# Layer 3 of a four-layer convolution kernel: one narrow mask for four heads, keys summed down the rows ahead of the scan on VectorE, q kept by rows as well

## The chip, the cores and the metric

One core of one Trainium2 chip runs the whole program in one launch. The metric is the device time of that core in microseconds. The kernel before took 3273.11 us, the median of three runs (3265.43 to 3276.16).

## The reference

The input x is 4 images of 256 channels by 48 by 48, all in f32. Four layers follow, each of them added to its own input, after a group normalisation over 32 groups:

- layer 0: a dilated 7x7 convolution to 128 channels, a 1x1 convolution to 49 maps, a softmax over them, and the weighted sum of the 49 shifted inputs;
- layer 1: a 3x3 convolution of the signs of the input with the signs of the weights;
- layer 2: a 3x3 convolution with weights rounded to three values;
- layer 3: linear attention in windows, in 8 heads of 32 channels. The change touches this layer alone.

```python
q = sigmoid(x Wq);  k = sigmoid(x Wk);  v = x Wv, each head's v divided by its norm
Ik  = integral(k)                   # sums over rows and columns
Ikv = integral(k[f] * v[g])
for w in (1, 2, 4):                 # window sizes 48, 24, 12
    wk  = box(Ik, 48 // w)          # the sum of k over the window about each point
    wkv = box(Ikv, 48 // w)
    attn = sum_d q[d] wkv[d, f]
    norm = sum_d q[d] wk[d]
    outs.append(attn / (norm + 1e-6))
out = Wout concat(outs) + bout
```

## The kernel before, in words

Layers 0 to 2 run image by image and fill the first 1390 us. Layer 3 begins as layer 2 of the last image ends, and projections of image 0 for it (`project_first`) already run beside that.

**The tiling of layer 3.** An image is cut into 6 bands of 8 rows (`RB`, `NRB`) and each band of keys into 3 squares of 16 columns (`KC`, `NKC`), so that a square of 8 by 16 keys fills 128 partitions. A block (`Block`) is one image b, one half `ct` of the channels (4 heads, `HG`) and one band of queries `rb`; `order` lists the 48 blocks, by image, then by half, then by band. One pass is the six blocks of one image and half. A block goes over the bands of keys that its widest window reaches, each in two halves of the columns (`tiles_of`): 8 to 12 tile steps for each block, 480 in all. Near steps, whose band of keys is at most one from the band of queries, are alternated with far ones.

**A tile step.** `scores` multiplies keys with queries on TensorE for four heads. The four heads make two pairs (`NPR`), each with a PSUM tile `s` of two banks. `masked` then makes the masked scores `sm` for up to three windows: `widest` (ScalarE, or VectorE for one pair of a far step) clips at zero, `middle` multiplies with the mask of the window of 24 on VectorE, and for near steps GpSimd (POOL) multiplies the result with the mask of the narrow window of 12. Before, each pair had its own `sm` tile (`room`, L1950), so that a near step had four narrow multiplications: two pairs by two key squares. Two steps later (`LAG`), `sums` multiplies the masked scores with v, into one accumulator for each window. `scores` and `sums` stand in TensorE's queue in the order scores of step n, sums of step n-2, side work, scores of step n+1.

**The norms.** `k_sums` (L1672), one job for each half of the channels, makes the windowed sums of the keys. It loads a band of keys `kf_d` into `kp`, whose rows are padded with zeros, runs a scan along the whole of it (two calls, `cs`), and takes for each window the difference of two shifted views (`pt`, three subtractions on VectorE). Then it sums down the rows: POOL adds to each row of `pt`, for all three windows at once, the row above (L1713 to L1719), carries the last row to the next band, and `pt` is stored to `kb_d`. `norms` loads two bands of such sums (`nhi`, `nlo`) and q (`nq`, from `q_d`), subtracts and multiplies by q on POOL, and sums over channels by a matmul; `ns` goes to `n_d`, is read back in another layout, inverted by `inverse` and stored to `r_d`.

**The end of a block.** `finish` stores the first half's result, `stage`, to `o_d`. For the second half `prepare` loads the first one's result as `o`, and the inverse norms, repeated over each head's channels, as `rc`, and multiplies `o` by `rc` on POOL; `finish` multiplies `stage` by `rc` on VectorE and applies `Wout`.

**Layouts.** Queries are held in the order (column, row), `p (w r)`, for the scores, and `q_d` has that order. Norms are computed in the order (row, column). So the q product in `norms` reads q with a stride of 8 elements, and both products with `rc` read `rc` with a stride of 48 elements.

**What sets the order.** All engines' calls stay in program order (`InOrder`). Side work (projections, `k_sums`, `norms`, `state`, `prepare`, `finish`) consists of generators that `advance` (L339) resumes once a step, in between two tile steps. A job that has POOL work first calls `pool_turn` (L369) with an estimated cost, `pool_op` (190 + 1.95 ns an element), and is put off while the step has no such time left. The main loop gives a step 3600 ns of it, less `far_time` (L2279), the estimate of that step's narrow masks. TensorE's time is given out likewise by `bank` and `turn`. `until` (L356) is otherwise: when something must be ready, such as block i-2 before block i begins, it calls `advance()` with no limit at all, over and over until it is:

```python
    def until(*keys):
        while not made.issuperset(keys):
            assert active
            advance()
```

Counters in `free` stand for buffers: one `cs`, two `o`, two `rc`.

Of the kernel before, what the change touches and what calls it, by code (L numbers as in the profile page):

```python
# [12 lines left out]
F32 = mybir.dt.float32  # L13
# [9 lines left out]
P = 128  # L23
# [4 lines left out]
RB = 8  # L28
# [219 lines left out]
def conv_preact_kernel(  # L248
# [71 lines left out]
    q_d = [dram.tile([C, HW], F32, tag=f"q{b}", name=f"q_d{b}") for b in range(B)]  # L320
    k_d = [dram.tile([C, HW], F32, tag=f"k{b}", name=f"k_d{b}") for b in range(B)]
# [105 lines left out]
    class Projection:  # L427
# [50 lines left out]
        def qk(self, g, a, name, mo):  # L478
# [26 lines left out]
            if name == "k":  # L505
                kt = self.scr.tile([P, NB], F32, tag="kt", name="kt")
                act.copy(kt.rearrange("p (c r x) -> p c r x", c=NKC, x=KC), rows)
            yield 1
            if name == "k":
                sync.dma_start(out=k_d[b][chans, cols], in_=kt)  # L510
            sync.dma_start(out=(q_d if name == "q" else kf_d)[b][chans, cols], in_=t)
# [1110 lines left out]
    with (  # L1622
# [4 lines left out]
        tc.tile_pool(name="smp", bufs=2 * (LAG + 1), reuse_waits="tile") as smp,  # L1627
# [27 lines left out]
        GAP = HALVES[0] + 1  # L1655
# [5 lines left out]
        carry = wts.tile([P, NCT, NW, W], F32, name="carry")  # L1661
# [10 lines left out]
        def k_sums(mo):  # L1672
# [14 lines left out]
            for at, (b, a) in enumerate(todo):  # L1687
# [3 lines left out]
                while step < loaded + FETCH + 1:  # L1691
                    yield 1
                yield from take("cs")
                cs = scr.tile([P, (RB + 1) * ROW], F32, tag="cs", name="cs", bufs=1)
                n = GAP + RB * ROW
                for i, j in ((0, n // 2), (n // 2, n)):
                    dve.tensor_tensor_scan(
                        cs[:, i:j],
                        kp[:, i:j],
                        kp[:, 0:1].to_broadcast([P, j - i]),  # L1700
                        cs[:, i - 1 : i] if i > 0 else 0.0,
                        ALU.add,
                        ALU.add,
                    )
                    yield 1
# [4 lines left out]
                for wi, h in enumerate(HALVES):  # L1710
                    dve.tensor_sub(pt[:, wi], shifted(cs, h - 1), shifted(cs, -h - 1))
                    yield 1
                free["cs"] += 1  # L1713
                for r in range(RB):
                    if r % 2 == 0:
                        yield from pool_turn(NW * W, 2)
                    if a > 0 or r > 0:
                        up = pt[:, :, r - 1, :] if r > 0 else carry[:, mo]
                        pool.tensor_add(pt[:, :, r, :], pt[:, :, r, :], up)  # L1719
                pool.tensor_copy(carry[:, mo], pt[:, :, RB - 1, :])  # L1720
                yield 1
# [8 lines left out]
        def norms(b, rb):  # L1730
# [4 lines left out]
            def load(ct):  # L1735
# [3 lines left out]
                qf = scr.tile([P, W, RB], F32, tag="nq", name="nq")  # L1739
                sync.dma_start(  # L1740
                    out=qf.rearrange("p w r -> p (w r)"),
                    in_=q_d[b][chans, rb * NB : (rb + 1) * NB],
                )
# [55 lines left out]
            act.copy(ns, ps[0 : D * NW, 0:NB])  # L1799
# [91 lines left out]
        class Block:  # L1891
# [48 lines left out]
            def masked(self, a, half, ss):  # L1940
# [9 lines left out]
                def room():  # L1950

                    t = smp.tile([P, SM_ROOM], F32, tag="sm", name="sm")
                    at, blocks_, views = 0, {}, {}
                    for wi in wis:
                        y0, y1 = rows_seen(wi, a, rb)
                        ps = self.parts(wi, a, half)
                        if wi == 0:
                            n = sum(p1 - p0 for _, p0, p1 in ps) * (y1 - y0)
                            block = t[:, at : at + 2 * n].rearrange("p (j n) -> p j n", j=2)
                            blocks_[wi] = block  # L1960
                            at, o = at + 2 * n, 0
                            for c, p0, p1 in ps:
                                m = (p1 - p0) * (y1 - y0)
                                views[wi, c] = block[:, :, o : o + m].rearrange(
                                    "p j (x r) -> p j x r", r=y1 - y0
                                )
                                o += m
                            continue
                        for c, p0, p1 in ps:
                            n = 2 * (y1 - y0) * (p1 - p0)  # L1970
                            views[wi, c] = t[:, at : at + n].rearrange(
                                "p (j x r) -> p j x r", j=2, r=y1 - y0
                            )
                            at += n
                    assert at <= SM_ROOM
                    return blocks_.get(0), views

                pairs = [room() for _ in ss]

                def times_mask(engine, wi, c, rows, cols, dst, src):  # L1980
# [5 lines left out]
                        dst, src, m.unsqueeze(1).to_broadcast([P, 2, ncol, nr])  # L1986
# [4 lines left out]
                def middle(s, room_):  # L1991
                    y0, y1 = rows_seen(1, a, rb)
                    for c, p0, p1 in parts_seen(1, half):
# [4 lines left out]
                        times_mask(dve, 1, c, (y0, y1), (p0, p1), room_[1][1, c], src)  # L1998

                def widest(engine, s, room_):  # L2000
                    n = room_[0].shape[2]
                    lo, hi = strip_columns(half) if full else (0, n)
                    if engine is act:
                        act.activation(room_[0], s[:, :, lo:hi], AF.Relu)
                    else:
                        dve.tensor_scalar_max(room_[0], s[:, :, lo:hi], 0.0)

                first, second = zip(ss, pairs)
# [42 lines left out]
            def sums(self, wi, a, half, sms):  # L2051
# [3 lines left out]
                for k, (c, p0, p1) in enumerate(self.parts(wi, a, half)):  # L2055
                    for j in range(HG):
# [5 lines left out]
                            sms[j // 2][wi, c][:, j % 2],  # L2062
# [24 lines left out]
        def prepare(i):  # L2087
# [34 lines left out]
        def finish(i, stage):  # L2122
# [156 lines left out]
        def far_time(i, a, half):  # L2279
# [4 lines left out]
            return 2 * sum(pool_op(2 * n) for n in columns(NW - 1, a, half, rb))  # L2284
# [79 lines left out]
```

## Time and profile before

| what | value |
|---|---|
| median of three runs | 3273.11 us |
| the profiled execution's own time | 3273.94 us |
| its span, first to last instruction | 3272.1 us |
| mean granted TensorE clock | 0.955 |
| layer 3, from its first accumulator on | 1402.2 to 3272.1 us |
| PE, DVE, ACT, POOL busy in layer 3 | 1723, 1097, 693, 1434 us of 1870 |
| POOL, narrow masks (`sm<-sm,masks`) | 1024 operations, 685.9 us |
| POOL, sums down the rows (`pt<-pt`, `pt<-pt,carry`, `carry<-pt`) | 188.0, 21.7 and 18.2 us |
| POOL, norms (`nhi<-nhi,nq`) and divisions (`o<-o,rc`) | 176.2 and 87.8 us |

A row of a tile's view reads: line, engine, operation, output<-inputs, count, then the shortest, the median and the longest duration in ns, and the first and last start in us. All instructions carry one line, since a helper records them; so tiles tell them apart. A row of the view by stretches gives the stretch in us, its length, then the busy time and count of PE (matmuls), PEld (weight loads), DVE (VectorE), ACT (ScalarE) and POOL (GpSimd), the granted clock, the share of DMA and GB/s. A row of the waits reads: who waited, for whom, how many us in total, how many times, and the longest.

### The profile page before, as it was taken

To read this page: it belongs to the slowest core of one execution; us is meant where nothing else is said; L and a number is where in the kernel's file an instruction comes from. 1 tells how busy PE (TensorE), PEld (TensorE's weight loads), DVE (VectorE), ACT (ScalarE), POOL (GpSimd) and SP (SyncE) were. 2 spreads that over 40 slices of the span, in tenths; PEclk is the share of its full clock that TensorE was granted. 3 is DMA by queue.
4 is the path that set the end of the run, shared out by engine and by line. 5 is a ranking of instruction groups with operands and counts; after the bars stand their busy time and mean duration, and the time that the engine had idled before them with its cause. 6 is when DMAs were issued, how large, how long until landed. Compare 5 with 4: busy or idle time off the path is not lost.

```text
span 3272.1 us, 98025 instructions
## 1 busy us (share of the span) xinstructions
PE 2902.1 (89%) x41802; PEld 2004.4 (61%) x41802; DVE 2017.0 (62%) x3907; ACT 963.2 (29%) x1894; POOL 1613.6 (49%) x2658
## 2 busy tenths in 40 slices
PE   3678999899899978889986879998999999999999
PEld 2456777678677756756553536564656655666665
DVE  7886578648856632656675636665556665655555
ACT  0002210111121053245431224442335532333332
POOL 0000021003002130358999968989857888844554
PEclk9889899999999978989998989999999999999999
DMA  8746513332341243144554645354543354511322
GB/s 269 222 152 186 168 47 128 112 121 83 103 155 57 90 148 121 61 128 131 170 173 136 178 145 160 118 170 138 159 123 126 126 162 149 164 40 41 87 75 68
DMA packets 373126, 424.46 MB, mean 130 GB/s; under 512 B 129075, under 2 KB 328531, under 8 KB 371539
## 3 DMA queue, kind: packets, MB, share of 16 engines
q1 hardware_dynamic: 371491, 416.32, 41.1%
q8 instruction: 331, 5.42, 0.7%
q0 software_dynamic: 144, 1.08, 0.2%
q14 instruction: 104, 0.85, 0.1%
q10 hardware_dynamic: 1056, 0.79, 0.1%
HBM read 287.91 MB, written 131.25 MB: 128 GB/s over the span
## 4 chain that ended last, share of the span: by engine, by line
PE 51%; POOL 16%; DVE 10%; DMA 3%; ACT 3%; issue 3%; SPq 1%; ACTq 0%; POOLq 0%; DVEq 0%
PE cv L244 15%; PE s L244 13%; PE acc L244 11%; POOL sm L244 6%; PE out_ps L244 5%; PE proj_ps L244 4%; POOL nhi L244 4%; POOL pt L244 3%; PE ap L244 2%; DVE sm L244 2%; DVE l2v L244 2%; ACT sm L244 2%; SPq L244 1%; DVE v L244 1%; POOL vu L244 1%
## 5 line engine op out<-in xcount | busy, mean ns | idle before, releaser
L244 DVE TENSOR_TENSOR sm<-s,masks 128x448 f32<-128x448 f32 (+11 forms) x1536 | 632.6, 468 | 443.7 <-PE s L244 417.3
L244 POOL TENSOR_TENSOR sm<-sm,masks 128x352 f32<-128x352 f32 (+11 forms) x1024 | 685.9, 702 | 363.9 <-DVE sm L244 263.1
L244 ACT ACTIVATE sm<-s 128x384 f32<-128x384 f32 (+2 forms) x864 | 470.5, 545 | 845.3 <-PE s L244 662.2
L244 PE MATMUL acc<-sm,vs 128*32 128x128 f32 (+20 forms) x17920 | 626.1, 279 | 36.4 <-POOL sm L244 31.7
L244 PE MATMUL cv<-vx,wt 128*128 128x288 f32 x2080 | 562.8, 427 | 88.6 <-DVE vx L244 50.3
L244 PE MATMUL s<-qs,ks 32*128 32x192 f32 (+3 forms) x7680 | 594.3, 401 | 41.6 <-ACT sm L244 36.3
L244 PEld LDWEIGHTS acc<-sm,vs 128*32 128x32 f32 x17920 | 431.6, 110 | 241.9 <-issue 139.0
L244 PEld LDWEIGHTS s<-qs,ks 32*128 32x128 f32 x7680 | 372.7, 186 | 271.1 <-issue 122.3
L244 PEld LDWEIGHTS cv<-vx,wt 128*128 128x128 f32 x2080 | 404.7, 199 | 211.3 <-issue 52.7
L244 POOL MEMSET v<- 128x16 f32 (+1 forms) x120 | 18.7, 216 | 744.7 <-DVE vx L244 628.3
L244 PE MATMUL cv<-v,wl 128*128 128x384 f32 x1152 | 226.4, 357 | 25.2 <-DVE x L244 8.1
L244 PEld LDWEIGHTS cv<-v,wl 128*128 128x128 f32 x1152 | 216.4, 197 | 36.4 <-issue 16.7
L244 DVE TENSOR_SCALAR sm<-s 128x896 f32<-128x896 f32 (+1 forms) x96 | 111.1, 1157 | 186.1 <-PE s L244 161.2
L244 POOL TENSOR_TENSOR pt<-pt 128x144 f32<-128x144 f32 x336 | 188.0, 560 | 25.2 <-DVE pt L244 1.0
L244 POOL TENSOR_TENSOR nhi<-nhi,nq 128x384 f32<-128x384 f32 x144 | 176.2, 1243 | 0.0
L244 PE MATMUL s<-masks 24*128 24x192 bf16 (+2 forms) x1920 | 172.1, 269 | 0.0
L244 POOL TENSOR_TENSOR v<-l2v,v 128x384 fp32r<-128x384 f32 x96 | 109.0, 1166 | 117.4 <-ACT v L244 108.7
L244 PE MATMUL cv<-pad,wl 128*128 128x384 bf16 x864 | 145.6, 331 | 4.2 <-ACT pad L244 4.2
L244 PE MATMUL out_ps<-o,wout_sb 128*32 128x384 f32 x1152 | 123.8, 499 | 7.4 <-DVE res L244 3.4
L244 PE MATMUL out_ps<-stage,wout_sb 128*32 128x384 f32 x1152 | 123.5, 498 | 6.2 <-DVE stage L244 6.2
L244 PEld LDWEIGHTS <-wl 128*128 128x128 bf16 x864 | 84.5, 98 | 64.7 <-issue 7.2
L244 DVE SCALAR_TENSOR_TENSOR res<-out_ps,bout_sb,res 128x384 f32<-128x384 f32 x48 | 42.1, 878 | 128.9 <-PE out_ps L244 128.8
(174 smaller groups left out, 3515.1 us busy)
## 6 DMA issues: line engine op xcount, KB each, us to landing
wt<-wt SPq DMA_DIRECT2D x48, 768.0 KB
kb_d<-pt SPq DMA_DIRECT2D x48, 576.0 KB
rc<-r_d SPq DMA_DIRECT2D x192, 144.0 KB
nhi<-kb_d SPq DMA_DIRECT2D x120, 192.0 KB
nlo<-kb_d SPq DMA_DIRECT2D x88, 192.0 KB
o_d<-stage SPq DMA_DIRECT2D x24, 576.0 KB
o<-o_d SPq DMA_DIRECT2D x24, 576.0 KB
wl<-wl_d SPq DMA_DIRECT2D x16, 768.0 KB
```

What stands on the lines that cost most here:

```text
L244: return lambda *args, **kwargs: self.tc.keep_in_program_order(op(*args, **kwargs))
```

## The change

Everything is in layer 3.

- **One `sm` tile for both pairs.** `room` is gone; a step has one tile of twice the size (`smp` has `LAG + 1` buffers instead of twice that many), with views over four heads. `middle` and `widest` write a pair's slice of it. The narrow mask is one multiplication for four heads for each key square: two in a near step instead of four. `far_time` follows.
- **Sums down the rows first.** In `k_sums`, VectorE adds to each row of the keys `kp` the row above (48 elements, eight additions a band, in two groups of four with a step between), and keeps the last row in `carry`. The scan multiplies its running sum by a mask `inside`, which is zero ahead of each row and one elsewhere, and adds the keys. The padding of a row is 24 elements instead of 25. Where the lower end of a window lies left of the image, `pt` is a copy of the scan, made by ScalarE (25, 13 and 7 of 48 columns); VectorE subtracts in the others. POOL's additions, its carry and their `pool_turn`s are gone.
- **q by rows as well.** `qk` makes a second copy of q on ScalarE, in the order (row, column), and stores it to the new `qr_d`; `norms` loads that, and its product is flat. The copy of the norms out of PSUM (`ns`) now turns them to (column, row), so that the products of `o` and `stage` with `rc` are flat too.

```diff
@@ qk
-            if name == "k":
-                kt = self.scr.tile([P, NB], F32, tag="kt", name="kt")
-                act.copy(kt.rearrange("p (c r x) -> p c r x", c=NKC, x=KC), rows)
+            kt = self.scr.tile([P, NB], F32, tag="kt", name="kt")
+            pattern = "p (r c x) -> p c r x" if name == "q" else "p (c r x) -> p c r x"
+            act.copy(kt.rearrange(pattern, c=NKC, x=KC), rows)
             yield 1
-            if name == "k":
-                sync.dma_start(out=k_d[b][chans, cols], in_=kt)
-            sync.dma_start(out=(q_d if name == "q" else kf_d)[b][chans, cols], in_=t)
+            first, second = (qr_d, q_d) if name == "q" else (k_d, kf_d)
+            sync.dma_start(out=first[b][chans, cols], in_=kt)
+            sync.dma_start(out=second[b][chans, cols], in_=t)
@@ layer 3's pools and constants
-        tc.tile_pool(name="smp", bufs=2 * (LAG + 1), reuse_waits="tile") as smp,
+        tc.tile_pool(name="smp", bufs=LAG + 1, reuse_waits="tile") as smp,
-        GAP = HALVES[0] + 1
+        GAP = HALVES[0]
-        carry = wts.tile([P, NCT, NW, W], F32, name="carry")
+        carry = wts.tile([P, NCT, W], F32, name="carry")
+        inside = wts.tile([P, (RB + 1) * ROW], F32, name="inside")
+        nc.gpsimd.memset(inside, 1.0)
+        for r in range(RB + 1):
+            nc.gpsimd.memset(inside[:, r * ROW + GAP - 1 : r * ROW + GAP], 0.0)
@@ k_sums
+                keys = shifted(kp, 0)
+                for r in range(RB):
+                    if a > 0 or r > 0:
+                        up = keys[:, r - 1] if r > 0 else carry[:, mo]
+                        dve.tensor_add(keys[:, r], keys[:, r], up)
+                    if r % 4 == 3:
+                        yield 1
+                dve.tensor_copy(carry[:, mo], keys[:, RB - 1])
                 yield from take("cs")
...
                     dve.tensor_tensor_scan(
                         cs[:, i:j],
+                        inside[:, i:j],
                         kp[:, i:j],
-                        kp[:, 0:1].to_broadcast([P, j - i]),
                         cs[:, i - 1 : i] if i > 0 else 0.0,
-                        ALU.add,
+                        ALU.mult,
                         ALU.add,
                     )
...
-                    dve.tensor_sub(pt[:, wi], shifted(cs, h - 1), shifted(cs, -h - 1))
+                    ahead_, behind_ = shifted(cs, h - 1), shifted(cs, 0)
+                    act.copy(pt[:, wi, :, : h + 1], ahead_[:, :, : h + 1])
+                    dve.tensor_sub(
+                        pt[:, wi, :, h + 1 :], ahead_[:, :, h + 1 :], behind_[:, :, : W - h - 1]
+                    )
                     yield 1
                 free["cs"] += 1
-                for r in range(RB):
-                    if r % 2 == 0:
-                        yield from pool_turn(NW * W, 2)
-                    if a > 0 or r > 0:
-                        up = pt[:, :, r - 1, :] if r > 0 else carry[:, mo]
-                        pool.tensor_add(pt[:, :, r, :], pt[:, :, r, :], up)
-                pool.tensor_copy(carry[:, mo], pt[:, :, RB - 1, :])
-                yield 1
@@ norms
-                sync.dma_start(
-                    out=qf.rearrange("p w r -> p (w r)"),
-                    in_=q_d[b][chans, rb * NB : (rb + 1) * NB],
-                )
+                sync.dma_start(out=qf, in_=qr_d[b][chans, rb * NB : (rb + 1) * NB])
...
-                    pool.tensor_mul(hi[:, wi], hi[:, wi], qf.rearrange("p w r -> p r w"))
+                    flat = hi[:, wi].rearrange("p r w -> p (r w)")
+                    pool.tensor_mul(flat, flat, qf)
...
-            act.copy(ns, ps[0 : D * NW, 0:NB])
+            act.copy(
+                ns.rearrange("p (w r) -> p r w", w=W),
+                ps[0 : D * NW, 0:NB].rearrange("p (r w) -> p r w", w=W),
+            )
@@ masked
-                    for _, views in pairs:
-                        for c, p0, p1 in parts_seen(2, half):
-                            src = views[1, c][
-                                :, :, p0 - seen1[c] : p1 - seen1[c], y0 - z0 : y1 - z0
-                            ]
-                            times_mask(pool, 2, c, (y0, y1), (p0, p1), views[2, c], src)
-                return [views for _, views in pairs]
+                    for c, p0, p1 in parts_seen(2, half):
+                        src = views[1, c][:, :, p0 - seen1[c] : p1 - seen1[c], y0 - z0 : y1 - z0]
+                        times_mask(pool, 2, c, (y0, y1), (p0, p1), views[2, c], src)
+                return views
@@ prepare
-                ow = o[:, wi].rearrange("p (w r) -> p w r", w=W)
-                pool.tensor_mul(ow, ow, rcs[0][:, wi].rearrange("p (r w) -> p w r", w=W))
+                pool.tensor_mul(o[:, wi], o[:, wi], rcs[0][:, wi])
@@ finish
-                sw = stage[:, wi].rearrange("p (w r) -> p w r", w=W)
-                dve.tensor_mul(sw, sw, rc[:, wi].rearrange("p (r w) -> p w r", w=W))
+                dve.tensor_mul(stage[:, wi], stage[:, wi], rc[:, wi])
@@ far_time
-            return 2 * sum(pool_op(2 * n) for n in columns(NW - 1, a, half, rb))
+            return sum(pool_op(4 * n) for n in columns(NW - 1, a, half, rb))
```

More of the change, by code (lines that the diff above doesn't have):

```diff
@@ L320, in conv_preact_kernel @@
     q_d = [dram.tile([C, HW], F32, tag=f"q{b}", name=f"q_d{b}") for b in range(B)]
+    qr_d = [dram.tile([C, HW], F32, tag=f"qr{b}", name=f"qr_d{b}") for b in range(B)]
     k_d = [dram.tile([C, HW], F32, tag=f"k{b}", name=f"k_d{b}") for b in range(B)]
@@ L1738, in load @@
                 lo = scr.tile([P, NW, RB, W], F32, tag="nlo", name="nlo")
-                qf = scr.tile([P, W, RB], F32, tag="nq", name="nq")
-                sync.dma_start(
-                    out=qf.rearrange("p w r -> p (w r)"),
-                    in_=q_d[b][chans, rb * NB : (rb + 1) * NB],
-                )
+                qf = scr.tile([P, NB], F32, tag="nq", name="nq")
+                sync.dma_start(out=qf, in_=qr_d[b][chans, rb * NB : (rb + 1) * NB])
                 for wi, h in enumerate(HALVES):
@@ L1948, in masked @@
                 left = {c: x0 for c, x0, _ in PARTS[half]}
[L1950 to L1956, printed above, removed]
-                        if wi == 0:
[L1958 to L1967, printed above, removed]
-                            continue
[L1969 to L1976, printed above, removed]
@@ L1978, in masked @@
-                pairs = [room() for _ in ss]
+                t = smp.tile([P, NPR * SM_ROOM], F32, tag="sm", name="sm")
+                at, blocks_, views = 0, [], {}
+                for wi in wis:
+                    y0, y1 = rows_seen(wi, a, rb)
+                    ps = self.parts(wi, a, half)
+                    for c, p0, p1 in ps:
+                        if wi == 0:
+                            continue
+                        n = HG * (y1 - y0) * (p1 - p0)
+                        views[wi, c] = t[:, at : at + n].rearrange(
+                            "p (j x r) -> p j x r", j=HG, r=y1 - y0
+                        )
+                        at += n
+                    if wi > 0:
+                        continue
+                    n = sum(p1 - p0 for _, p0, p1 in ps) * (y1 - y0)
+                    block = t[:, at : at + HG * n].rearrange("p (j n) -> p j n", j=HG)
+                    blocks_ = [block[:, 2 * pr : 2 * pr + 2] for pr in range(NPR)]
+                    at, o = at + HG * n, 0
+                    for c, p0, p1 in ps:
+                        m = (p1 - p0) * (y1 - y0)
+                        views[wi, c] = block[:, :, o : o + m].rearrange(
+                            "p j (x r) -> p j x r", r=y1 - y0
+                        )
+                        o += m
@@ L1980, in times_mask @@
+                assert at <= NPR * SM_ROOM
                 def times_mask(engine, wi, c, rows, cols, dst, src):
@@ L1985, in times_mask, with middle @@
                     engine.tensor_mul(
-                        dst, src, m.unsqueeze(1).to_broadcast([P, 2, ncol, nr])
+                        dst, src, m.unsqueeze(1).to_broadcast([P, dst.shape[1], ncol, nr])
                     )
                 many = seen(NW - 1, a, rb)
-                def middle(s, room_):
+                def middle(s, pr):
                     y0, y1 = rows_seen(1, a, rb)
@@ L1997, in middle, with widest @@
                         )[:, :, :, y0:y1]
-                        times_mask(dve, 1, c, (y0, y1), (p0, p1), room_[1][1, c], src)
-                def widest(engine, s, room_):
-                    n = room_[0].shape[2]
+                        dst = views[1, c][:, 2 * pr : 2 * pr + 2]
+                        times_mask(dve, 1, c, (y0, y1), (p0, p1), dst, src)
+                def widest(engine, s, pr):
+                    dst = blocks_[pr]
+                    n = dst.shape[2]
                     lo, hi = strip_columns(half) if full else (0, n)
                     if engine is act:
-                        act.activation(room_[0], s[:, :, lo:hi], AF.Relu)
+                        act.activation(dst, s[:, :, lo:hi], AF.Relu)
                     else:
-                        dve.tensor_scalar_max(room_[0], s[:, :, lo:hi], 0.0)
-                first, second = zip(ss, pairs)
+                        dve.tensor_scalar_max(dst, s[:, :, lo:hi], 0.0)
+                first, second = zip(ss, range(NPR))
                 if full:
@@ L2061, in sums @@
                             kvs[self.b, self.ct, a][1][:, c, j, :],
-                            sms[j // 2][wi, c][:, j % 2],
+                            sms[wi, c][:, j],
                             start=(wi == 0 and (a, half) == todo[0] and k == 0),
```

## The prediction

> **What bounds the kernel now.** I read the page's totals and forty slices first, then the busy times by stage, then the engines' waits, then single tiles.
>
> ```profile
> span 3272.1 us, 98025 instructions
> PE 2902.1 (89%) x41802; PEld 2004.4 (61%) x41802; DVE 2017.0 (62%) x3907; ACT 963.2 (29%) x1894; POOL 1613.6 (49%) x2658
> PE   3678999899899978889986879998999999999999
> POOL 0000021003002130358999968989857888844554
> ```
>
> POOL's 49% is an average over two different programs. Up to slice 16 (layers 0 to 2) it is almost idle; in layer 3 it runs at 8 or 9 tenths, and PE dips where POOL is at 9. So I cut layer 3 into its eight passes (four images, two channel halves each), at the first clearing of the accumulators of each pass:
>
> ```profile
> core 0: us, PE busy (x) PEld busy (x) DVE busy (x) ACT busy (x) POOL busy (x), PEclk, DMA share, GB/s
> 1402.20:1627.90 225.70, 214.17 (x4813) 137.61 (x4812) 144.70 (x289) 114.75 (x230) 185.39 (x348) 0.97 0.43 135
> 1627.90:1944.70 316.80, 253.19 (x4585) 142.24 (x4584) 181.85 (x313) 79.40 (x158) 282.68 (x390) 0.92 0.54 158
> 1944.70:2166.50 221.80, 214.64 (x4616) 133.23 (x4608) 138.59 (x279) 105.29 (x209) 189.26 (x330) 1.00 0.47 141
> 2166.50:2416.60 250.10, 225.82 (x4594) 137.50 (x4592) 145.08 (x267) 78.12 (x159) 217.33 (x301) 0.97 0.55 161
> 2416.60:2630.50 213.90, 211.97 (x4646) 132.47 (x4639) 134.27 (x279) 108.17 (x216) 157.73 (x317) 1.00 0.37 117
> 2630.50:2868.60 238.10, 221.42 (x4526) 137.17 (x4528) 140.89 (x261) 74.27 (x148) 207.47 (x279) 0.98 0.54 158
> 2868.60:3056.50 187.90, 177.86 (x3975) 124.55 (x3968) 97.24 (x208) 67.90 (x134) 82.57 (x139) 1.00 0.13 42
> 3056.50:3272.00 215.50, 203.87 (x4198) 126.72 (x4196) 114.61 (x226) 64.72 (x124) 111.53 (x158) 1.00 0.28 81
> ```
>
> Matmul counts hardly differ, lengths do. The passes with 158 us of POOL or less are PE-bound (213.9 long, 212.0 busy). **The floor** of the others follows: between passes 5 and 7 a matmul is worth (213.9-187.9)/(4646-3975) = 0.0387 us. First-half floors are then 220, 213, 213; second-half floors start from the last pass (215.5 less some 6.5 of tail) plus 0.0387 per matmul more: 224, 224, 222. Against that the six passes lie 5, 93, 9, 26, 1 and 16 us too high: **150 us**.
>
> Most of it stands in three places, where a `begin` waits in the planner for an unfinished block (`until`) and the waiting steps are given out with no budget, so queued side jobs of POOL run one after another with no tile between them:
>
> ```profile
> 1747.00:1786.00 39.00, 20.91 (x235) 7.09 (x234) 17.01 (x21) 2.65 (x6) 36.90 (x44) 0.78 0.50 141
> 1900.30:1948.00 47.70, 29.69 (x264) 9.82 (x268) 9.14 (x11) 5.51 (x12) 29.16 (x31) 0.71 0.47 140
> 2233.00:2260.00 27.00, 15.99 (x150) 5.19 (x150) 6.95 (x11) 1.46 (x4) 25.77 (x37) 0.75 0.24 69
> ```
>
> POOL is busy 92 of these 114 us; the second also holds one 11 us wait for a load of key sums. PE's waits in layer 3 name the same owners, narrow masks and norms:
>
> ```profile
> PE acc L244 <- POOL sm L244: 31.7, 52, 2.1
> PE norm_ps L244 <- POOL nhi L244: 29.5, 18, 10.8
> ```
>
> [...] about half the operations that start with POOL in flight take longer:
>
> ```profile
> L244 DVE TENSOR_TENSOR pt<-cs x144: 541/644/1605, 1416.2 to 2703.5; 128x384 f32<-128x384 f32 x144
> L244 POOL TENSOR_TENSOR pt<-pt x336: 482/497/1074, 1418.4 to 2718.0; 128x144 f32<-128x144 f32 x168
> L244 DVE TENSOR_SCALAR nr<-nr x24: 184/471/1184, 1613.8 to 2873.5; 128x72 f32<-128x72 f32 x24
> ```
>
> [...] the trace's undisturbed ones are 541 to 550. [...] Here the q product (one operand strided by 32 bytes) has a median of 1197 ns against 1000 for the flat subtraction of the same size: 20%.
>
> **The change, part by part.** *Taken from POOL.* The row sums: 376 additions of 128x144 at 209.7 us (188.0+21.7) and 48 copies at 18.2: 228. Narrow masks, 1024 operations into 512 of twice the size: over their twelve sizes the medians lie on 0.22 us + 1.91 ns per element, so the fixed part goes 512 times: 114. The flat q product: 144 x 0.197 = 28. The flat o product: 72 x (1.244-1.039, the mean of the subtraction) = 15. Together 385 of POOL's 1434 us in layer 3; 1049 remain, 59% of some 1790. The planner follows: each row sum no longer asks it for four turns of two `pool_op(144)` (48 x 3.77 = 181 us of its units), and `far_time` gives back 0.38 per near step; norms and `prepare` are thus given out earlier.
>
> *Where that gain lies.* Of the 150 us I leave 35: the start's 5, and 10 at the end of each of three images, where `finish` is bound by its two `rc` buffers, its loads and its bank rather than by POOL (image 2, with POOL least loaded, still has such waits). Gain **115**; ends 45 (below) and 145.
>
> *Put on VectorE.* 376 additions of 128x48, each needing the one before. Not in the trace: [...] 0.195 taken, and 0.034 between dependent operations (the gap between the two on nr). The POOL lock adds 0.20 per `pt<-cs` now (mean 743 against 545); with POOL at 59% instead of 77% I take 0.16, bounds 0 and 0.31. So 376 x 0.389 = 146 us, less 360 of 1152 elements of the subtractions (18) and the flat division (72 x (0.804-0.541) = 19), plus 48 carry copies at most 0.2 (9): net +118 on 1097, 68% of layer 3. That it isn't the bound on average doesn't make it free: VectorE's queue also carries the middle masks (2.16 us per near step), and scores of the next tile wait for their banks. Behind a held addition are these masks, then PE's scores and POOL's narrow masks. I cut layer 3 at the first score matmul of each of its 480 tile steps: near steps (key rows at most one tile from the query rows) in which POOL isn't the bound are 0.15 to 0.4 us longer than a bare one with 0.3 to 2 us of side work on VectorE, without a trend, and 1.4 us longer with 2 to 3 (six steps). Four additions take 1.56. The two halves' `k_sums` take `cs` by turns of five steps, so one such group falls beside a scan (0.95): 2.5, 0.5 over, and one beside a subtraction (0.45): 2.0, 0.15 over. 48 x 0.65 = **31 us** on the path; bounds 0 (POOL idle) and 61 (a wait of 0.25).
>
> *The scan* multiplies by a mask instead of adding a constant: both forms have two inputs and one feedback; taken as unchanged (0.78 undisturbed), at worst +0.2 x 96 = 19 on VectorE, a gain excluded as no element is saved. *The narrow mask's new wait*: it starts after both pairs' middle masks, about 1.1 us later, but takes 2.6 instead of 3.0 and is read two steps (7 us) on: 0, at most 0.1 x 256 = 26 if POOL is still behind. *ScalarE* gets 144 copies of 200, 104 and 56 elements (0.34, 0.25, 0.20 on the line through 96 at 0.239 and 384 at 0.512): 38 us, and 48 q copies at 0.512: 25, twelve of them in layer 2. They wait for the scan, given out a step earlier, and stand ahead of the next tile's widest mask. Their cover is ScalarE's 662 us of waiting for scores; 0 taken, 29 if 0.2 of each of 144 shows. *The queues*: 48 more stores on SP at 0.36 = 17 us, ahead of the q store and whatever loads follow; SPq is 1% of the chain: 1. The `ns` copy now writes strided: 24 x at most 0.3 = 7, before a two-step DMA way; 2. The mask `inside` costs ten memsets on POOL at layer 3's start (0 to 3 us): 1. The wider `sm` tile is released by the same matmuls as its halves were: 0.
>
> **Sum**: -115 + 31 + 4 (queues 1, `ns` 2, `inside` 1) = -80. The profiled execution took 3273.94 (span 3272.1 plus 1.8 outside), 0.8 above the median of 3273.11 of the three runs. 3273.9-80 = 3194, stated as **3195**.
>
> **Rivals.** *All cover* (0.15): VectorE's additions hide and only the start and a third of the image ends remain: -150+15+4 = -131, 3143. For it: POOL at 59%, steps with 1.9 us of side work at normal length. Against: in-order queue behind the masks.
> *The unpaced stretches stay* (0.13): they come from the order of `finish` (an o, two rc's, one bank), not from POOL's load. For it: stretches occur at each image's end, even where POOL is light. Then only 25 of the other 36 us go and 20 of the 114 (the row sums and fixed costs in them): 45-31-4 = -10, 3264.
> *VectorE's additions become the bound* (0.10): both halves' groups fall into the same steps, eight additions each behind a POOL operation: at 0.40 of wait 8 x 0.63 = 5.0 us, 3.0 above the 2 that a step bears, in 24 x 2 steps: +144, against 111 gained: 3307. It decides from 2.3 us extra in each of these 48 steps on, a wait of 0.31 per addition. For it: waits up to 1.06 on `pt<-cs`. Against: means of 0.2, and the shared `cs` keeps the halves apart.
>
> **Numbers.** Forecast 0.62 (3150 to 3235 its own), rivals 0.15, 0.13, 0.10. 0.3% is 10 us, about what a measurement tells from no change. The third rival is faster in half its cases (0.05) and the same in half (0.08); slower 0.09, the fourth's rest the same: faster 0.82, same 0.09, slower 0.09. The range 3125 to 3262 leaves out the fourth, half the third, some tails: 0.2.
>
> **What would show it.** Right: POOL under 65% in layer 3; the second pass of image 0 near 240 instead of 317; PE's waits on narrow masks and norms below a third; additions of 0.2 to 0.5. Wrong: stretches of 25 us and more with few matmuls; score waits for VectorE or ScalarE grown by over 60; additions above 0.54.

## The result and the profile after

The kernel after took 3255.53 us (median of 14 runs, 3247.75 to 3272.15), the kernel before 3271.53 us (14 runs) beside it: ratio 0.9947, interval 0.9929 to 0.9965. It is 16 us faster; 78 were forecast. The time lies near the upper end of the stated range (3125 to 3262) and outside the forecast's own 3150 to 3235. The profiled execution of after has a span of 3257.5 us.

The page of after, the same lines as before:

```profile
span 3257.5 us, 97465 instructions
PE 2887.8 (89%) x41802; PEld 2014.4 (62%) x41802; DVE 2212.3 (68%) x4331; ACT 1033.4 (32%) x2086; POOL 1252.9 (38%) x1732
PE   3678999898899968989988889999999999999999
POOL 0000021003002130325577556667745567734443
```

POOL lost 361 us and its 8s and 9s are gone. But PE shows 8s (slices 21 to 24) where POOL is at 5 to 7: POOL's load no longer explains PE's gaps. VectorE gained 195 us.

The first six of the eight passes of layer 3 in after (stretch, length, busy times as before):

```profile
1408.50:1646.20 237.70, 221.91 (x4814) 142.10 (x4812) 181.66 (x393) 129.57 (x275) 125.79 (x195) 0.96 0.46 145
1646.20:1923.90 277.70, 231.94 (x4576) 141.74 (x4572) 231.26 (x417) 87.39 (x194) 180.53 (x191) 0.93 0.56 162
1923.90:2163.80 239.90, 223.67 (x4600) 139.20 (x4596) 186.02 (x361) 117.62 (x244) 147.06 (x199) 0.96 0.51 155
2163.80:2398.20 234.40, 221.29 (x4617) 138.42 (x4620) 156.66 (x296) 85.29 (x175) 174.84 (x207) 0.99 0.60 172
2398.20:2620.80 222.60, 215.47 (x4644) 135.12 (x4636) 167.15 (x357) 121.58 (x252) 113.95 (x191) 1.00 0.39 125
2620.80:2853.10 232.30, 216.28 (x4523) 135.09 (x4525) 156.68 (x289) 78.30 (x160) 163.87 (x169) 0.99 0.56 161
```

The second passes of images 0 to 2 fell from 316.8, 250.1 and 238.1 to 277.7, 234.4 and 232.3: 61 us gained. The first ones rose from 225.7, 221.8 and 213.9 to 237.7, 239.9 and 222.6: 39 us lost, in passes that were almost at their floor. Layer 3 also begins 7 us later: the first score matmul starts at 1399.3 instead of 1392.2.

The waits in layer 3. First after, then two of before that grew:

```profile
PE s L244 <- ACT sm L244: 78.9, 105, 6.2
PE s L244 <- DVE sm L244: 13.1, 11, 2.6
PE norm_ps L244 <- POOL nhi L244: 1.1, 1, 1.1
ACT sm L244 <- DVE sm L244: 204.1, 269, 6.0
```

```profile
PE s L244 <- ACT sm L244: 36.3, 94, 1.9
ACT sm L244 <- DVE sm L244: 135.1, 283, 3.3
```

PE's waits for POOL's masks (31.7 before) and norms (29.5) are all but gone. In their place PE waits for a bank of scores that ScalarE has not read yet, and ScalarE, whose order is that of the program, waits for VectorE. The longest such wait grew from 3.3 to 6.0 us. What VectorE does there is in the view of the tile `kp` (shortest/median/longest ns):

```profile
L244 DVE TENSOR_TENSOR kp<-kp x336: 173/210/1529, 1417.1 to 2672.2; 128x48 f32<-128x48 f32 x168
L244 DVE COPY carry<-kp x48: 154/560/1502, 1424.1 to 2674.3; 128x48 f32<-128x48 f32 x48
L244 DVE TENSOR_TENSOR kp<-kp,carry x40: 175/710/1467, 1439.0 to 2664.4; 128x48 f32<-128x48 f32 x40
```

The median of the first row hides two groups. Sorting its 336 by whether a POOL operation was in flight at the start: 154 with POOL idle have a median of 208 ns, 182 with POOL busy one of 758, and in those POOL had 0.61 us left on average. The mean of all 376 additions is 0.481 us. Of these, 147 start with more than 0.3 us of POOL's operation left, and each of the 147 ends 61 to 70 ns after that operation. One group in the timeline (start, us), VectorE and then POOL:

```profile
1702.03 2.30 DVE L244 TENSOR_TENSOR kp<-kp 128x48 f32<-128x48 f32 x4
1704.26 0.34 DVE L244 TENSOR_TENSOR pt<-cs 128x184 f32<-128x184 f32 x1
1704.52 1.08 DVE L244 TENSOR_SCALAR sm<-s 128x896 f32<-128x896 f32 x1
```

```profile
1701.68 2.09 POOL L244 TENSOR_TENSOR sm<-sm,masks 128x336 f32<-128x336 f32 x2 [0.26 <-DVE sm L244]
```

Four additions worth 0.9 us take 2.30 beside two narrow masks: the first lasts 598 ns and the second 1167, each ending 67 ns after a mask of POOL, the third 208. The widest mask (1704.52) queues behind them.

### The profile page after: what moved, and what is told of

Its sections match the earlier page's. It is cut to its first block, busy times and chain, and to the rows that moved or that the text cites. A ratio compares the mean times of both kernels' runs of the same rounds, so it can differ in the third digit from the quotient of the medians.

```text
span 3257.5 us, 97465 instructions
## 1 busy us (share of the span) xinstructions
PE 2887.8 (89%) x41802; PEld 2014.4 (62%) x41802; DVE 2212.3 (68%) x4331; ACT 1033.4 (32%) x2086; POOL 1252.9 (38%) x1732
## 4 chain that ended last, share of the span: by engine, by line
PE 57%; DVE 19%; ACT 5%; DMA 3%; issue 2%; POOL 2%; SPq 1%; ACTq 0%; DVEq 0%; POOLq 0%
PE s L244 15%; PE cv L244 15%; PE acc L244 13%; DVE sm L244 5%; PE out_ps L244 5%; PE proj_ps L244 4%; DVE kp L244 3%; PE ap L244 2%; ACT sm L244 2%; DVE l2v L244 2%; DVE cs L244 2%; DVE v L244 1%; POOL nhi L244 1%; SPq L244 1%; DVE x L244 1%
## 5 line engine op out<-in xcount | busy, mean ns | idle before, releaser
L244 POOL TENSOR_TENSOR sm<-sm,masks 128x704 f32<-128x704 f32 (+11 forms) x512 | 596.3, 1186 | 736.5 <-DVE sm L244 735.8
L244 PE MATMUL s<-qs,ks 32*128 32x320 f32 (+3 forms) x7680 | 617.6, 403 | 95.7 <-ACT sm L244 78.9
L244 PE MATMUL acc<-sm,vs 128*32 128x128 f32 (+20 forms) x17920 | 613.8, 281 | 5.7 <-issue 5.6
L244 PEld LDWEIGHTS s<-qs,ks 32*128 32x128 f32 x7680 | 386.4, 186 | 340.8 <-ACT sm L244 155.5
L244 PE MATMUL s<-masks 24*128 24x192 bf16 (+2 forms) x1920 | 181.9, 270 | 0.2 <-issue 0.2
L244 DVE TENSOR_TENSOR kp<-kp 128x48 f32<-128x48 f32 x336 | 154.9, 462 | 9.7
L244 POOL TENSOR_TENSOR nhi<-nhi,nq 128x384 f32<-128x384 f32 x144 | 148.2, 1049 | 0.0
L244 DVE TENSOR_TENSOR vx<-v 128x868 f32<-128x868 f32 x112 | 115.3, 1055 | 0.5
```

Of the source, the lines that this page charges most:

```text
L244: return lambda *args, **kwargs: self.tc.keep_in_program_order(op(*args, **kwargs))
```

## The experiments

Layer 3 alone means the time from the first score matmul to the end, in the profiled execution.

**The additions, the masks, both.** x_noadds drops the additions and the carry copy:

```diff
-                        up = keys[:, r - 1] if r > 0 else carry[:, mo]
-                        dve.tensor_add(keys[:, r], keys[:, r], up)
...
-                dve.tensor_copy(carry[:, mo], keys[:, RB - 1])
```

> The changed kernel, but the additions of the key rows and the copy to carry are left out (the windowed sums of the keys are then wrong); everything else, the steps between included, stays. Theory (the additions wait for POOL, and the masks behind them wait with them): VectorE loses 209 us of its queue, ScalarE's wait for VectorE falls from 204 to about 130 us, and the time falls by 60 us, to about 3195. Rival (the gain went into the planner's unpaced stretches, the additions are hidden): at most 10 us less, about 3246.

x_nonarrow makes no narrow mask:

```diff
-                        src = views[1, c][:, :, p0 - seen1[c] : p1 - seen1[c], y0 - z0 : y1 - z0]
-                        times_mask(pool, 2, c, (y0, y1), (p0, p1), views[2, c], src)
+                        views[2, c] = views[1, c][:, :, p0 - seen1[c] : p1 - seen1[c], y0 - z0 : y1 - z0]
```

> The changed kernel, but the narrow masks on POOL are left out (the third window then takes the second one's masked scores); the additions stay. Theory (POOL's mask stands in VectorE's way): the mean of a key addition falls below 0.30 us and the time by about 60 us, to 3195. Rival (additions cost by their number): the mean falls too, but the time falls by at most 20 us, to 3235.

x_nonarrow_noadds has both edits:

> Both left out: the additions of the key rows with their carry, and POOL's narrow masks. Theory (the additions cost because of the masks): hardly less than without the masks alone, 5 to 15 us, about 3185. Rival (by their number): another 45 us less than without the masks alone, about 3190 from 3235.

Measured: x_noadds 3165.76 us (ratio to before 0.9669, 0.9642 to 0.9697), x_nonarrow 3179.85 (0.9725, 0.9701 to 0.9748), both 3137.53 (0.9582, 0.9555 to 0.9609). So the additions cost 3255.5-3165.8 = 90 us where the joined masks run, and 3179.9-3137.5 = 42 where there are none: 48 us exist only when both are there. The first two theories had the right sign and too small a size (60 us each; the mean addition in x_nonarrow is 0.322 us, not below 0.30). The third, 5 to 15 us without masks, was wrong, and its rival's 45 close. But the rival's reason, the number of operations, isn't shown by that: without masks 135 of the 376 additions still start while POOL does other work (norms, divisions). The passes of x_noadds:

```profile
1420.80:1641.60 220.80, 215.08 (x4817) 138.18 (x4820) 150.35 (x287) 130.10 (x275) 128.44 (x196) 0.97 0.50 156
1641.60:1888.60 247.00, 224.87 (x4571) 138.81 (x4571) 185.92 (x311) 87.70 (x194) 181.12 (x190) 0.94 0.63 182
1888.60:2104.00 215.40, 212.59 (x4600) 132.30 (x4594) 149.59 (x283) 117.72 (x244) 148.99 (x199) 1.00 0.57 174
2104.00:2332.80 228.80, 220.20 (x4624) 136.96 (x4624) 141.91 (x267) 85.14 (x175) 175.73 (x207) 0.99 0.60 175
2332.80:2546.10 213.30, 211.82 (x4644) 132.80 (x4636) 139.81 (x278) 121.92 (x252) 114.03 (x191) 1.00 0.40 130
2546.10:2769.40 223.30, 215.11 (x4526) 135.12 (x4528) 143.24 (x262) 78.36 (x160) 164.78 (x169) 0.98 0.58 167
```

Against the prediction's floors (220, 224, 213, 224, 213, 222) these lie 1, 23, 2, 5, 0 and 1 us too high: 32 of the 150. The same six passes of after lie 18, 54, 27, 10, 10 and 10 too high: 129.

**The length of the POOL operation.** x_split is after with the narrow mask made for each pair again:

```diff
-                    for c, p0, p1 in parts_seen(2, half):
-                        src = views[1, c][:, :, p0 - seen1[c] : p1 - seen1[c], y0 - z0 : y1 - z0]
...
+                    for pr in range(NPR):
+                        for c, p0, p1 in parts_seen(2, half):
+                            js = slice(2 * pr, 2 * pr + 2)
+                            src = views[1, c][:, js, p0 - seen1[c] : p1 - seen1[c], y0 - z0 : y1 - z0]
...
```

> The changed kernel, but the narrow mask is again one multiplication for each pair, four in a near step instead of two; the order of the side work stays. POOL gets 512 more operations, some 110 us more. Theory (what hurts is how long one POOL operation keeps VectorE's two-input operations out): the mean of a key addition falls from 0.48 to below 0.40 us, and the time falls by about 10 us, to 3245. Rival (the number of VectorE's operations hurts, whatever POOL does): the additions keep their mean, and the time stays within 5 us or rises by up to 10.

x_halfcols cuts each joined mask by columns instead: as short as in x_split, but begun only when both pairs' middle masks are done.

```diff
-                        src = views[1, c][:, :, p0 - seen1[c] : p1 - seen1[c], y0 - z0 : y1 - z0]
-                        times_mask(pool, 2, c, (y0, y1), (p0, p1), views[2, c], src)
+                        mid = (p0 + p1) // 2
+                        for x0, x1 in ((p0, mid), (mid, p1)):
...
+                            times_mask(pool, 2, c, (y0, y1), (x0, x1), dst, src)
```

> The changed kernel with its narrow mask for four heads cut by columns instead of by pairs: each key square in two operations of half the columns, so that an operation is as short as with one for each pair, but none starts before both pairs' middle masks are done. Theory A (the length of one POOL operation decides): as with one mask for each pair, 3205 to 3220. Theory B (the later start decides, because it pushes POOL's work into the time of VectorE's side work): as the changed kernel, 3245 to 3265.

Measured: x_split 3211.42 (0.9813, 0.9794 to 0.9831), x_halfcols 3222.22 (0.9857, 0.9829 to 0.9886). Undoing one part of the change makes it 44 us faster, though POOL is then busy 74 us more. In x_split the theory had the right sign and far too small a size (10 us); in x_halfcols the theory of length came within 2 us of its range. 33 of the 44 go with the length alone; the other 11 could be the later start, and lie at the edge of the intervals. The masks' mean falls from 1186 to 693 and 691 ns; in the page of x_split:

```profile
L244 POOL TENSOR_TENSOR sm<-sm,masks 128x352 f32<-128x352 f32 (+11 forms) x1024 | 675.0, 693 | 608.7 <-DVE sm L244 374.0
```

The additions' mean falls from 0.481 to 0.409 (x_split) and 0.446 (x_halfcols), and to 0.322 in x_nonarrow.

**Waiting or occupancy.** In x_oneinput each of the 424 operations reads one SBUF input:

```diff
-                        up = keys[:, r - 1] if r > 0 else carry[:, mo]
-                        dve.tensor_add(keys[:, r], keys[:, r], up)
+                        dve.tensor_reduce(
+                            junk, keys[:, r].rearrange("p (n m) -> p n m", m=6), AX.X, ALU.add
+                        )
...
```

> The changed kernel with each key addition and each copy to carry replaced by a VectorE reduction of the same 48 elements into a scratch tile: as many operations in the same places, but with one SBUF input (the sums down the rows are left out). Theory (it is the exclusion of two-input operations and POOL's operations that costs): the operations last 0.2 us whatever POOL does, and the time lies near that without additions, 3165 to 3190. Rival (so many more operations in VectorE's queue cost by their number and their gaps): near the changed kernel, 3235 to 3255.

Measured 3178.95 us (0.9713, 0.9683 to 0.9744), inside the theory's range. Their row in the view of the tile `junk`:

```profile
L244 DVE TENSOR_REDUCE junk<-kp x424: 170/203/205, 1416.7 to 2602.7; 128x8 f32<-128x48 f32 x142
```

None exceeds 205 ns, beside the same joined masks, though 321 of them start with POOL in flight. So of the 90 us, 13 (3178.95-3165.76, at the edge of the intervals) come with 424 operations of 0.2 us on VectorE, and some 77 go when the waits for POOL go. One thing differs besides: the reductions do not depend on each other. VectorE's queue shows no cost of that: between two neighbours in a group lie 34 ns in both kernels (283 gaps in each).

**Another way to sum the rows.** x_colscan is x_split with the keys loaded by columns, so that one addition of the carry and one scan of 384 elements replace the eight additions, and ScalarE copies the result into `kp`. The sigmoid then writes k by columns too, and the next band is loaded only after `pt` is stored:

```diff
...
+                if a > 0:
+                    dve.tensor_add(by_row[:, 0], by_row[:, 0], carry[:, mo])
+                dve.tensor_tensor_scan(raw, below, raw, 0.0, ALU.mult, ALU.add)
+                yield 1
+                act.copy(shifted(kp, 0), by_row)
+                act.copy(carry[:, mo], by_row[:, RB - 1])
...
```

> Narrow masks for each pair again, and the eight additions of a band replaced: the keys are loaded by columns, one addition of 48 elements takes in the carry, one scan of 384 elements sums down the rows of all columns, and ScalarE copies the result into the padded rows. VectorE's two-input operations for a band fall from 13 to 7. Theory (each such operation pays for POOL's operation in flight, and the masks behind it wait): 25 to 45 us below the kernel with one mask for each pair (3211), about 3176. Rival (only the additions' bare time counts; the scan costs 0.95 against their 1.6): 10 us below, about 3200.

> Sums down the rows by one scan over columns, as before, but with the joined narrow masks. Theory (long POOL operations cost in proportion to the number of VectorE's two-input operations; with 7 a band instead of 13 the joining loses about half as much as it did): 15 to 30 us above the kernel with the same scan and one mask for each pair (3200), about 3222. Rival (joining relieves POOL and costs nothing once the additions are gone): 3175 to 3200.

Measured: x_colscan 3199.88 (0.9787, 0.9758 to 0.9815), where the theory was wrong and the rival's number right: some 11 us below x_split, whose interval overlaps. Fewer operations had been priced as if they were all that mattered; the scan meets POOL too, and ScalarE gained a copy:

```profile
L244 DVE TENSOR_TENSOR_SCAN pt<-below,pt x48: 947/1237/1683, 1434.8 to 2633.9; 128x384 f32<-128x384 bf16 x48
L244 ACT COPY kp<-pt x48: 878/908/953, 1438.1 to 2637.3; 128x384 f32<-128x384 f32 x48
```

What the missing gain went to, these two or the later load, was not separated. j_colscan, with joined masks: 3224.41 (0.9842, 0.9814 to 0.9871), 24 above x_colscan and inside the theory's 15 to 30. Joining costs here too, about half of the 44; that it goes by the number of VectorE's two-input operations rests on these two points alone.

**The other parts alone, in the kernel before.** b_join joins the masks and nothing else, b_q takes q by rows and the flat products and nothing else. Both put the change's lines for that part into the kernel before.

> The kernel before with the joined narrow mask alone. POOL's busy time falls by some 110 us, and its masks are twice as long. Theory A (long POOL operations hold up VectorE's scans, subtractions and divisions): the gain from POOL's load is eaten, 3255 to 3275. Rival (POOL's load is the bound of this kernel and the joining gives 512 fixed costs back): 3230 to 3240.

> The kernel before with q by rows and the flat products alone. POOL loses 43 us of work, ScalarE gains 48 copies, twelve of them beside layer 2. Theory (the copies of q in layer 2 delay its chain by some 7 us, as in the changed kernel; the rest gains 10 to 20): 3255 to 3268. Rival (copies hidden): 3245 to 3255.

Measured: b_join 3223.09 (0.9855, 0.983 to 0.988), 48 us faster than before; the theory, which saw the gain eaten up, was wrong, and the gain is even above the rival's (3230 to 3240). In this kernel, where POOL is busy 1437 us of layer 3, 512 fixed parts less are worth more than the longer waits they cause (a `pt<-cs` takes 0.915 us on average instead of 0.743). b_q is 3259.59 (0.996, 0.9948 to 0.9973), 11 us faster and inside the theory's range: layer 3 alone is 20 us shorter in the profile (1859.8 against 1879.9), but starts 12 later.

**The sums on POOL.** p_sums keeps everything of after but the engine, and asks the planner for a turn of POOL:

```diff
+                    if r % 4 == 0:
+                        yield from pool_turn(W, 4)
...
-                        dve.tensor_add(keys[:, r], keys[:, r], up)
+                        pool.tensor_add(keys[:, r], keys[:, r], up)
...
-                dve.tensor_copy(carry[:, mo], keys[:, RB - 1])
+                pool.tensor_copy(carry[:, mo], keys[:, RB - 1])
```

> The changed kernel, narrow masks joined, with the key additions ahead of the scan made by POOL instead of VectorE (48 elements each instead of the 144 of the kernel before), and a turn asked of the planner for them. POOL gets 376 operations of some 0.31 us, 117 in all, less than half of what the sums cost it before; VectorE loses 209 us. Theory (two-input operations on VectorE are what is dear, POOL has room at 59 to 66% busy): 3175 to 3205. Rival (POOL is the bound as soon as it carries sums and masks): 3220 to 3260.

p_sums_split also has x_split's edit:

> The kernel after with both edits: POOL adds the keys ahead of the scan (48 elements, as in p_sums), and the narrow mask is one per pair again, four in a near step. It tells whether the joined mask is bad by itself or only beside VectorE's additions. Theory (a collision of two edits: a longer POOL operation costs where a chain of short VectorE operations with two SBUF inputs stands behind it; elsewhere joining saves 512 fixed parts of POOL): with no additions left on VectorE, joining is a gain as it was in the kernel before (48 us), though a smaller one since POOL is less loaded than there, so this kernel is 10 to 48 us slower than p_sums: 3195 to 3233 beside a kernel before of 3273. Rival (the long operation holds back VectorE's other two-input work as well, the subtractions and divisions, so that splitting pays in any case): no slower than p_sums, 3185 or less.

Measured: p_sums 3185.43 us (0.9732, 0.9708 to 0.9757): 70 us below after, inside the theory's range, and with p_sums_split the fastest of the kernels here that compute all of the reference. An addition of 48 elements takes POOL 287 ns (median) instead of 497 for 144, and no score matmul waits for POOL, though it is the slower engine for it. From p_sums, the tile `kp` and three of PE's waits (the largest other one is 16.2 us, two waits for ScalarE's sigmoid of a projection):

```profile
L244 POOL TENSOR_TENSOR kp<-kp x336: 277/287/811, 1426.3 to 2605.9; 128x48 f32<-128x48 f32 x168
```

```profile
PE s L244 <- ACT sm L244: 29.3, 77, 2.4
PE norm_ps L244 <- POOL nhi L244: 10.8, 6, 6.7
PE acc L244 <- POOL sm L244: 5.5, 7, 1.3
```

p_sums_split took 3189.51 us (0.9745, 0.97 to 0.9789), which cannot be told from p_sums. The theory (10 to 48 slower) missed; the rival's number missed by 4 us, and its claim, no slower, isn't excluded. With no chain of additions on VectorE the joined mask shows no harm, and no gain either, within some 15 us.

## Why the prediction was wrong

**The gain, right.** 115 us were to come out of the 150. x_noadds, which has all of the change but the additions, is 117 us shorter than before in layer 3 alone (1879.9 to 1762.5), and 32 us are left where 35 were kept back. The rival in which the unpaced stretches stay is wrong in the main: around 1747 matmuls run again (612 in 40 us, where 235 stood in 39), and the second stretch shrank from 47.7 to 26.5 us. With its few matmuls that one is still among the forecast's signs of being wrong:

```profile
1740.00:1780.00 40.00, 31.11 (x612) 19.41 (x608) 33.72 (x62) 11.55 (x25) 26.74 (x26) 0.91 0.62 178
1900.50:1927.00 26.50, 17.87 (x236) 7.52 (x232) 16.64 (x25) 5.50 (x13) 17.31 (x18) 0.81 0.59 174
```

Of the signs of being right, the second pass of image 0 failed: 277.7 us, not near 240; without the additions it is 247.0. The share foreseen for POOL, 59% of layer 3, came out as 1074 of 1849 us, 58%. The narrow masks gave back 90 us of POOL's busy time (685.9 to 596.3) rather than 114, though counted by durations, which overlap, it is 112 (1024 x 0.702 less 512 x 1.186); the q product 28 as forecast (its median is 1005 instead of 1197 ns).

**The failed step: VectorE's additions, 31 us on the path.** Their bare duration was right: 208 ns (median with POOL idle), where 0.195 us had been taken, the author's estimate. An estimate from the trace of before comes to 0.192: its shortest `pt<-cs` takes 541 ns for 384 elements, and its middle masks of 114 and of 432 elements take 267 and 597 ns (medians), so 1.04 ns an element for the 336 fewer. The term that failed is the wait for POOL, "0.16, bounds 0 and 0.31": it was 0.481-0.195 = 0.29. It was scaled down from 0.20 because POOL's *load* was to fall from 77 to 59%. But the same change made the mean narrow mask longer (1186 ns instead of 702), and an addition that meets POOL ends only when POOL's operation has ended: 0.61 us were left of it here, 0.36 on average for `pt<-cs` before. Load alone would have it the other way round: in x_split POOL is busy 64% of layer 3 instead of 58, with masks of 693 ns, and the wait is 0.409-0.195 = 0.21. Put into the prediction's own rule, 0.29 makes a group of four last 4 x (0.195+0.034+0.29) = 2.1 us, 1.0 over what a step bears beside a scan (0.95) and 0.5 beside a subtraction (0.45): 48 x 1.5 = 72 us instead of 31. (By that rule the forecast's own 2.0 beside a subtraction is 0 over and not 0.15: 25 us, not 31.) Measured: 90 at the medians, 96 in layer 3 alone (1762.5 to 1858.3). What makes up the rest stays open; the 48 copies to `carry`, priced at 0.2 us at most, took 0.58 on average. The prediction's joining of the masks was charged with its later start only; what it does to VectorE stood in no term. The rival in which the additions hide failed at the same step.

That it is a wait and not occupancy, x_oneinput shows: same count, same length, same masks, 77 us less. The wait already stood in the trace of before: of the 128 `pt<-cs` that start with POOL in flight, 97 (the prediction has about half) take longer than any with POOL idle (at most 550 ns), and of the 61 with over 0.3 us of POOL's operation left, 57 end 410 to 418 ns after that operation. A held addition outlasts POOL's operation by 61 to 70 ns and not by its own 208, so that the wait is what is left less some 0.14 us. Middle masks, which have one operand in PSUM, kept their mean (468 ns before, 467 after). VectorE's other work with two SBUF inputs paid as well: the flat division was to save 19 us and saved 2 (84.9 to 83.0), the shorter subtractions 18 and saved 3 (107.0 to 104.1), and the scan took 14 more (93.9 to 108.3). With a mask for each pair (x_split) the three take 53.8, 84.6 and 96.1.

**Where the loss reaches PE.** Forecast as the sign of being wrong: score waits for VectorE or ScalarE grown by over 60. They grew from 36.8 (36.3+0.5) to 92.0 us (78.9+13.1): 55, just below it. In x_noadds they are 38.2. So 54 of the 96 us are score waits. PE's other idle time in layer 3 has 11 more; for the remaining 31 PE is busy longer with the same matmuls (1720 against 1689 us, at a granted clock of 0.97 against 0.98), and why isn't shown. The rival in which VectorE's additions become the bound had, with "a wait of 0.31 per addition", almost the size of the wait (0.29), but not its place: it put eight additions into each of 48 steps, and of the 93 groups that stand between two of VectorE's score masks in the trace, 90 have three or four.

**q's copies ahead of layer 3, taken as 0.** They were to be hidden by ScalarE's waits for scores, but the first dozen lie in layer 2, where no scores are waited for. They are also slower than the 0.512 taken: the 48 of k take 511 to 514 ns, those of q, which read with a stride of 8 elements, 877 to 927 (x_colscan's copy of 384 elements into `kp`, which reads with the same stride, 878 to 953):

```profile
L244 ACT COPY kt<-sg x96: 511/696/927, 1157.3 to 2587.8; 128x384 f32<-128x384 f32 x96
```

From the first to the twentieth sigmoid of image 0 the two profiles without q copies take 118 (before) and 112 us (b_join); the ten that have after's q and k projections take 120 to 130, on average 126. Their first score starts at 1397 to 1412, against 1392 and 1384. But the granted clock of that stretch differs as well: it is 0.93 in b_join, 0.86 before, and from 0.88 (120 us) to 0.81 (130 us) in the ten. At the same 0.86, x_split takes 124.4 against the 118.2 of before: some 6 us of the 11 go with the copies, whose twelve add 11 us to ScalarE there; the rest goes along with the clock. Whether the copies have a part in the clock, and by which wait they act, was not tried. Two small terms of the prediction besides: the `ns` copy, which now writes with a stride of 8 elements, takes 857 ns (median) instead of 475, 0.38 us more where at most 0.3 had been taken; the ten memsets of `inside` lie within 1.1 us of POOL.

**The sum again**, for the profiled executions: -117 (gain in layer 3) +96 (additions) +7 (later start) = -14; the spans differ by 14.6. These are single executions: among the kernels with q's copies the start alone varies by 15 us. Joining alone brings 48, q by rows 11, sums and q without joining 60 (x_split); the sums alone were not run. Together they bring 16, since joining and the additions work against each other.

## What to carry to other kernels

What it cost here to move short two-input operations from GpSimd to VectorE went by the length of GpSimd's remaining operations, not by its load alone: the share of starts that meet one, times what is then left of it, less what the operation does meanwhile. In after, 209 of the 376 additions met one, with 0.63 us left: 0.56 x (0.63-0.14) = 0.27 us, and the mean was 0.27 above the 0.208. Edits that relieve one bound should be measured singly and in pairs; here the best step was to shrink the work (48 elements instead of 144) and leave it on GpSimd, for whose norms and masks PE then waits 16 us in all. A copy "hidden" on an engine needs its cover checked in every stage in which it is issued.

## What the runs showed of the hardware

- A VectorE addition of 48 elements with two SBUF inputs takes 208 ns (median) with POOL idle and 758 with POOL in flight (after); a one-input reduction of the same 48 elements never more than 205 ns (x_oneinput).
- A held addition ends 61 to 70 ns after the operation of POOL that held it, whatever was left of that (all 147 of after with over 0.3 us left). A division of 384 elements was held through four and five operations of POOL that followed each other without a gap: 4.16 and 5.27 us in after, where the shortest takes 0.53.
- Of the 1164 middle masks of before that start with POOL in flight, none is over 30 ns longer than the median with POOL idle of its size; they have one operand in PSUM.
- A plain VectorE copy of 48 elements waits too: 154 ns at its shortest, 560 in the median, 1502 at most; at most 200 had been taken for it. The 26 of the 48 that start with over 0.3 us of POOL's operation left end 41 to 49 ns after it.
- ScalarE's copy of 384 elements takes 511 to 514 ns for k and 877 to 927 for q, which it reads with a stride of 8 elements (after).
